# Second decoder layer: output products behind the row copies, absolute sums one per turn, next rows transposed behind the scores

## The chip, the cores and the metric

The kernel runs on one core of a Trainium2 chip. The metric is the device time of one execution in microseconds (us); of several executions the median is given. Besides the times there is a profile of one execution: for each instruction its engine, start, duration and what it waited for. The engines are PE (TensorE, matrix products and transposes), DVE (VectorE), ACT (ScalarE), POOL (GpSimd) and SP (SyncE, which here only issues DMA transfers). Each engine works through its own list of instructions in order; engines wait for each other by semaphores.

## The reference

Two decoder layers on `x` of 16 batches x 112 tokens x 512 values in float32. Each layer adds to `x` a self attention, a cross attention and a feed-forward part, each on the layer-normalized `x`:

```
x = x + L0_attn(ln(x));  x = x + L0_xattn(ln(x), ctx);       x = x + L0_ffn(ln(x))     # mixture of 8 experts + shared
x = x + L1_attn(ln(x));  x = x + L1_xattn(ln(x), ctx, ctx);  x = x + L1_ffn(ln(x))
```

The change lies mainly in the second layer. Its self attention has 16 heads of 32 values, biases and a causal mask. Its cross attention has one head of 512: the queries of a batch attend to 375 context rows and to keys and values made from the batch's own 112 rows. Its feed-forward part quantizes its weights to three values first, and needs for that the mean of each whole matrix's absolute values:

```
scale = mean(|W|) + 1e-8;  q = clip(round(W / scale), -1, 1) * scale
hidden = silu(x @ up.T) * (x @ gate.T);  out = hidden @ down.T
```

## The kernel before

The program is seven stages, one per part (the self- and cross-heads of the first layer's cross attention are two): `stage_attn0`, `stage_fp8_self`, `stage_fp8_cross`, `stage_moe`, `stage_attn1`, `stage_cross1`, `stage_ffn`. `x` stays on chip as 14 tiles of 128 token rows. A recording layer takes every instruction with what it reads and writes, gives it buffers, sets the order on each engine by a model of its own and adds the waits. `manual_schedule` fixes the order on the named engines to the order of the code; `issue_after(i)` puts instructions behind `i` on `i`'s engine only.

**Weights.** One pool of 12 pieces of 128 x 2048 float32 (1 MB, `new_piece`, `load_piece`, L106 to L114) holds every stage's weights, the key tiles `w_kt` of attention 1, and the pieces `w_sum` whose absolute values are summed.

**End of the MoE stage** (L1620 to L1636). While PE runs the shared expert on the last six row tiles, POOL issues 28 gathers (`yg`, L1468, through a tile with five buffers) of the experts' results, and VectorE adds them into `x` (L1634). VectorE's order is fixed here: three additions per step, between the shared expert's own instructions (`h`, L1506, and the addition of its product, L1517). SP meanwhile issues the weights of attention 1 and cross attention 1, and then the pieces for the absolute sums.

**Absolute sums.** `Ternary.add_up(q)` loads three pieces and has ScalarE sum their absolute values (L1835). `stage_attn1` calls it four times before its attention, with the loads placed behind the previous stage's last load on SP (`behind`). The sums are read at the start of `stage_cross1` (`scales`).

**Self attention** (`narrow_attention`, used by both layers). The work is cut into blocks (of 4 batches in attention 1, of 2 to 4 tiles in attention 0) and these into quads: all heads of one batch, or of one tile of 128 rows. The loop has a turn `n` per quad, and one more. In a turn PE computes the scores of quad `n` (L212, L219), VectorE their extremes (`nq_m`, L226), ScalarE the exponentials in four parts `r` (L234), POOL the division (L239); and for quad `n - 1` PE transposes the probabilities (L246), ScalarE copies them out (`ptt`, L251) and PE multiplies them by the values (L259). Between the four parts of a turn stand steps of other work, in the list `now`: a share of the next block's preparation (`before`: transposes of its normalized rows, then query, key and value products), and the two half products of quad `n - 2` with the output weights (`after`), which are put in the middle of the list:

```
now[len(now) // 2 : len(now) // 2] = after
```

PE's and ScalarE's orders are fixed. In the first turn of a block (`group == 0`) two of the next block's row transposes stand ahead of the scores; the rest begin the list. From the second block on, these transposes use the same two PSUM buffers (`mm`) as the products. A transposed row tile is copied out of PSUM by VectorE (`xt`, L190), which also normalizes the rows (`xn`, L145, two buffers, so the third row tile is normalized after the first is transposed).

**Cross attention 1** (`stage_cross1`). For each of four blocks: normalize and transpose its rows (`block_xt`), query and key products for four batches (L1757), and then batch by batch value products (L370), scores (L1780, L1784), a softmax over one row of 487 (maximum L1099, exponentials L1100, division L1791), transposes of the probabilities (L1795), products with context and values (L1805, L1808) and, where a tile of `x` is complete, the output product (L370) and its addition (L1816). The block's transposed rows have one buffer. No engine's order is fixed in this stage. The row transposes and the transposed probabilities share two PSUM buffers (`tr`).

Of the kernel before, what the change touches and what calls it, by code (L numbers as in the profile page):

```python
# [26 lines left out]
GB = 4  # L27
NB = B // GB
# [8 lines left out]
FQ = 4  # L37
# [42 lines left out]
def rows_of(k, g):  # L80

    t = 7 * (g // 2)
    if g % 2:
        rows = [(t + 3, P // 2, P // 2)] + [(t + i, 0, P) for i in (4, 5, 6)]
    else:
        rows = [(t + i, 0, P) for i in range(3)] + [(t + 3, 0, P // 2)]
    return [(k.x[:, t], r, n) for t, r, n in rows]
# [18 lines left out]
def new_piece(k, what, dt=F32):  # L106

    return k.wpool.tile([P, PIECE], dt, tag="w", name=f"w_{what}", bufs=PIECES)


def load_piece(k, what, src):
    piece = new_piece(k, what)
    k.piece_load = k.nc.sync.dma_start(out=piece[:, : src.shape[-1]], in_=src)
    return piece  # L114
# [10 lines left out]
def behind(k):  # L125


    return k.tc.issue_after(k.last_load.ins)
# [30 lines left out]
def block_xt(k, wk, rows):  # L159

    steps = NormedRows(k, wk, rows)
    for i in range(len(rows)):
        steps.transpose(i)
    return steps.xt
# [119 lines left out]
def narrow_attention(k, blocks, aside=None):  # L284

    quads = [(block, group) for block in blocks for group in range(block.groups)]  # L290
    k.evictions = []
    last = len(quads) - 1
    with k.tc.manual_schedule(engines={mybir.EngineType.PE, mybir.EngineType.Activation}):
        for _, step in blocks[0].before(("tr", "mm")):
            step()
        todo, made, done = [], [], 0
        for n in range(len(quads) + 1):
            now = []
            if n <= last:
                block, group = quads[n]  # L300
                if group == 0:
                    done += 1


                    if n == 0:
                        with k.tc.issue_after(k.evictions[2].ins):
                            todo = blocks[done].before(("mm", "tr"))
                    elif done < len(blocks):
                        with k.tc.issue_after(k.xt_copy.ins):
                            todo = blocks[done].before(("mm",))  # L310

                        for _ in range(2):
                            todo.pop(0)[1]()
                    else:
                        todo = []
                budget = sum(cost for cost, _ in todo) / (block.groups - group)
                while todo and (budget > todo[0][0] / 2 or group == block.groups - 1):
                    now.append(todo.pop(0))
                    budget -= now[-1][0]
                made.append(block.quad(group))  # L320
                made[n].scores()

            ahead = n > 0 and done == len(blocks) and not todo and not now
            if n > 1:
                after = quads[n - 2][0].after(quads[n - 2][1])
                now[len(now) // 2 : len(now) // 2] = after
            total, used = sum(cost for cost, _ in now), 0.0
            for r in range(4):
                if ahead:
                    for i in ((0, 1), (2,), (3,), ())[r]:  # L330
                        made[n - 1].transpose_probs(i, ("tr", "mm")[i % 2], i > 1)
                elif n:
                    made[n - 1].transpose_probs(r)
                if n <= last:
                    made[n].exponentials(r)
                while now and used + now[0][0] / 2 < total * (r + 1) / 4 + 1.0:
                    used += now[0][0]
                    now.pop(0)[1]()
                if n:
                    made[n - 1].values(r)  # L340
            for _, step in now:
                step()
            if aside:
                with k.tc.issue_after(k.xt_copy.ins):
                    aside()
        block, group = quads[-1]
        for _, step in block.after(group):
            step()
# [213 lines left out]
class Weights:  # L562
# [56 lines left out]
    def step(self, count):  # L619
        self.ends()  # L620
        self.begin(count)
        self.centers()
        return self
# [1015 lines left out]
class Attn1Block:  # L1639
# [5 lines left out]
    def before(self, tags=("tr",)):  # L1645

        k, wk, nc = self.k, self.wk, self.k.nc
        wq, wkk, wv, _ = (chunks(w, 0, KC, D) for w in k.weights["attn1"])
        rows = rows_of(k, self.g)
        normed = NormedRows(k, wk, rows, tags)  # L1650
        self.qt = wk.tile([P, 4, NT], F32, tag="qt", name="qt", bufs=2)
        self.kt = chunks(new_piece(k, "kt"), 0, 4, NT)
        self.vn = {}

        def transpose(i):
            normed.transpose(i)
            if i == len(rows) - 1:
                for x, first, n in rows:
                    r = slice(first, first + n)
                    nc.gpsimd.tensor_tensor(x[r], x[r], self.bias[r, 1, :], ALU.add)  # L1660

        def wide(dst, w, g, at, sign):
            def product(ps, c):
                nc.tensor.matmul(  # L1664
                    ps, w[:, c, g * P : (g + 1) * P], normed.xt[:, c, :], start=c == 0, stop=c == 3
                )

            def then(ps):
                k.evictions.append(nc.vector.tensor_scalar(
                    dst[:, g], ps, k.vec[:, at + g : at + g + 1], sign / math.sqrt(math.sqrt(32.0)),  # L1670
                    ALU.add, ALU.mult,
                ))

            steps = halves_of(k, [P, NT], "mm", "ps_q", product, then)
            return [(2.0 * NT, step) for step in steps]

        def values(i):
            def product(pv, c):
                nc.tensor.matmul(  # L1679
                    pv, normed.xt[:, c, i * S : (i + 1) * S], wv[:, c, :], start=c == 0, stop=c == 3  # L1680
                )

            def then(pv):
                self.vn[i] = wk.tile([S, D], F32, tag="vn", name="vn", bufs=7)
                nc.vector.tensor_tensor(self.vn[i], pv, self.bias[:S, 0, :], ALU.add)

            return [(2.0 * D, step) for step in halves_of(k, [S, D], "mm", "ps_v", product, then)]

        steps = [(6.0 * n, lambda i=i: transpose(i)) for i, (_, _, n) in enumerate(rows)]
        for g in range(4):  # L1690
            steps += wide(self.qt, wq, g, V_BQ, -1.0)
        for g in range(4):
            steps += wide(self.kt, wkk, g, V_BK, 1.0)
        for i in range(GB):
            steps += values(i)
        return steps
# [33 lines left out]
def stage_attn1(k):  # L1730
    with k.stage("s4", mm=2, tr=1, acc=1, quad=4) as wk:
        mask_to_bf(k, wk, causal_mask(k, wk, S))
        rows = wk.tile([P, 2, D], F32, tag="rows", name="rows")
        k.nc.sync.dma_start(out=rows, in_=k.a["attn1_rows"].partition_broadcast(P))
        with behind(k):
            for q in range(FQ):
                k.ternary.add_up(q)
        at = {}
        narrow_attention(k, [Attn1Block(k, wk, g, rows, at) for g in range(NB)])


def stage_cross1(k):
# [3 lines left out]
    with k.stage("s5", mm=3, tr=2, sc=2, acc=1) as wk:  # L1746
        k.ternary.scales(wk)
        todo, tiles = [(q, m) for q in (0, 1) for m in range(3)], {}
        for g in range(NB):
            xt = block_xt(k, wk, rows_of(k, g))  # L1750
            qt = wk.tile([P, KC, NT], F32, tag="qt", name="qt")
            kt = wk.tile([P, KC, NT], F32, tag="kt", name="kt")
            for n, (dst, w) in enumerate(((qt, wq), (kt, wkk))):
# [11 lines left out]
            for i in range(GB):  # L1765
# [23 lines left out]
                exp_rows(k, pr, ps, sums)  # L1789
                nc.vector.reciprocal(sums, sums)  # L1790
                nc.vector.tensor_scalar(pr, pr, sums, None, ALU.mult)  # L1791
                pt = k.psum.tile([CC, 4, S], F32, tag="tr", name="ps_pt", bufs=2)
                for ch in range(4):
                    n = CC if ch < NCH else S
# [24 lines left out]
class Ternary:  # L1819
# [2 lines left out]

    def __init__(self, k, pool):
        self.k, self.w = k, {}
        self.sums = pool.tile([P, 3, FQ], F32, tag="t_sums", name="t_sums")
        self.s = pool.tile([P, 3], F32, tag="t_s", name="t_s")
        self.half = pool.tile([P, 2, 3], F32, tag="t_half", name="t_half")
# [1 line left out]
    def part(self, q, m):  # L1829
        return self.k.a["ffn_w"][q][:, PIECE * m : PIECE * (m + 1)]  # L1830

    def add_up(self, q):
        for m in range(3):
            w = load_piece(self.k, "sum", self.part(q, m))
            self.k.nc.scalar.activation(w, w, AF.Abs, accum_out=self.sums[:, m, q : q + 1])  # L1835

    def scales(self, wk):
        nc = self.k.nc
# [275 lines left out]
```

## Time and profile before

| | us |
|---|---|
| median of 3 runs (lowest, highest) | 3747.02 (3745.94, 3757.47) |
| the profiled execution's own time | 3740.01 |
| its span, first to last instruction | 3738.2 |
| PE, DVE, ACT, POOL busy in the span | 3577.4, 1798.3, 1425.7, 928.1 |
| last product of the MoE stage ends | 2732.55 |
| turns of attention 1 | 2785.8 to 3056.3 |
| first products of cross attention 1 | 3061.5 |

A line of the timeline reads: start, length, engine, line, operation, output<-inputs, sizes, and how many instructions were merged; in brackets the idle time of the engine before them, and what ended it (`<-` engine, output and line). A line of the table of windows gives the stretch, its length, and then busy time (and instructions) of PE, PE's weight loads, DVE, ACT and POOL, the granted PE clock as a share of full speed, the DMA engines' mean busy share, and GB/s. A line of the chain of waits gives start, length, and the engine or transfer on which the end depended then. PE is busy nearly all the time, so the idle times in front of its instructions are what to read; idle time of other engines costs nothing by itself.

### The profile page before, as it was taken

Reading aid. Unit: us, or ns where it says so; the run is one execution under the profiler, and the core shown is the slowest. Engines: PE = TensorE matmul, PEld = TensorE weight load, DVE = VectorE, ACT = ScalarE, POOL = GpSimd, SP = SyncE. Lnnn points to the kernel's source line nnn. Section 1 sums busy time; section 2 is a strip of 40 time slices with the busy share of each in tenths; the row PEclk is TensorE's granted clock in tenths of the full one; section 3 lists DMA queues with packets and bytes.
Section 4 is the critical chain, followed back from the end, with each engine's and each line's share of the span. In section 5 each row is a group of like instructions: output and inputs, shape, how many; then the busy total and the mean of one; then the engine's idle time right before and its main releaser. Section 6 shows DMA issues by size and latency. Waiting matters only on the chain.

```text
span 3738.2 us, 46258 instructions
## 1 busy us (share of the span) xinstructions
PE 3577.4 (96%) x16450; PEld 2315.5 (62%) x16450; DVE 1798.3 (48%) x3888; ACT 1425.7 (38%) x4133; POOL 928.1 (25%) x1314
## 2 busy tenths in 40 slices
PE   8888899999999999999999999999989999999999
PEld 4546788886666666566666654555544445556888
DVE  5557777876556444544445542111244453214333
ACT  3546766554444444444444430111124431112222
POOL 2335555554222222322222210000232220000000
PEclk9999999999999999999999999999989999999999
DMA  2144333432212111211121115999830022222000
GB/s 88 56 145 150 125 105 118 155 113 87 61 56 73 59 44 51 73 49 49 42 84 44 50 40 165 317 317 319 298 124 12 1 79 78 74 77 82 12 12 17
DMA packets 118117, 364.56 MB, mean 98 GB/s; under 512 B 13280, under 2 KB 33248, under 8 KB 108720
## 3 DMA queue, kind: packets, MB, share of 16 engines
q1 hardware_dynamic: 105504, 332.20, 27.2%
q0 software_dynamic: 5040, 16.52, 1.2%
q10 hardware_dynamic: 7344, 12.89, 0.9%
q8 instruction: 131, 2.15, 0.2%
q14 instruction: 98, 0.80, 0.1%
HBM read 317.09 MB, written 44.47 MB: 97 GB/s over the span
## 4 chain that ended last, share of the span: by engine, by line
PE 70%; DVE 9%; POOL 5%; ACT 3%; issue 2%; DMA 2%; POOLq 0%; SPq 0%; ACTq 0%; DVEq 0%
PE ps_kv L1157 14%; PE ps L1551 6%; PE ps_av L1214 4%; PE ps_s L1189 3%; PE ps_y L1569 3%; PE ps_q L718 3%; PE ps_acc L718 3%; PE ps_u L1933 3%; PE ps_o L370 3%; PE ps_o L1915 3%; PE ps_q L1664 3%; PE ps_g L1933 3%; PE ps_p L1757 3%; PE ps_pt L1204 2%; PE ps_v L1679 1%
## 5 line engine op out<-in xcount | busy, mean ns | idle before, releaser
L1157 PE MATMUL ps_kv<-w_kv,ct 128*125 128x512 f32 x1408 | 636.7, 593 | 0.0
L1157 PEld LDWEIGHTS ps_kv<-w_kv,ct 128*125 128x125 f32 x1408 | 261.9, 188 | 281.8 <-issue 246.9
L559 POOL TENSOR_TENSOR r_o<-r_t,r_m 128x64 fp32r<-128x64 bf16 (+6 forms) x224 | 148.0, 679 | 323.9 <-DVE r_t L557 297.5
L1551 PE MATMUL ps<-w_expert,xgt 128*128 128x448 f32 x560 | 216.4, 539 | 0.7 <-ACT xgt L1543 0.7
L1100 ACT ACTIVATE pr<-ps_s,ex_m 112x375 f32<-112x375 f32 (+1 forms) x272 | 157.4, 580 | 153.9 <-DVE ex_m L1099 145.9
L540 POOL TENSOR_SCALAR cu_v<-cu_v 125x2 f32<-125x2 f32 (+1 forms) x248 | 48.7, 196 | 620.8 <-DVE cu_v L1133 620.8
L541 POOL TENSOR_TENSOR cu_v<-cu_v,mhalf 125x2 f32<-125x2 f32 (+1 forms) x248 | 190.3, 767 | 20.5
L1133 DVE TENSOR_REDUCE cu_v<-sq 125x2 f32<-125x256 f32 (+1 forms) x248 | 118.0, 477 | 160.2 <-ACT sq L1132 160.2
L239 POOL TENSOR_TENSOR pr<-pr,nq_s 112x448 f32<-112x448 f32 (+1 forms) x120 | 118.9, 992 | 291.9 <-DVE nq_s L238 222.7
L234 ACT ACTIVATE pr<-ps_s,nq_m 112x112 f32<-112x112 f32 (+1 forms) x480 | 167.1, 378 | 56.8 <-DVE nq_m L226 56.7
L1099 DVE TENSOR_REDUCE ex_m<-ps_s 112x1 f32<-112x375 f32 (+1 forms) x272 | 148.7, 548 | 79.1 <-PE ps_s L1784 67.1
L1189 PE MATMUL ps_s<-kt,qt 128*112 128x375 f32 x512 | 183.3, 479 | 1.6 <-ACT pr L1100 1.1
L1132 ACT ACTIVATE sq<-ps_kv 125x256 f32<-125x256 f32 x176 | 67.6, 384 | 268.5 <-PE ps_kv L1157 186.5
L534 ACT ACTIVATE qt<-ps_t,turned 128x448 f32<-128x448 f32 (+6 forms) x224 | 116.6, 581 | 130.0 <-PE ps_t L1173 121.9
L1551 PEld LDWEIGHTS ps<-w_expert,xgt 128*128 128x128 f32 x560 | 103.6, 190 | 92.0 <-issue 91.0
L1214 PE MATMUL ps_av<-pt,vn 125*128 125x224 f32 x768 | 159.6, 356 | 0.2
L1189 PEld LDWEIGHTS ps_s<-kt,qt 128*112 128x112 f32 x512 | 90.0, 177 | 100.9 <-issue 60.1
L1214 PEld LDWEIGHTS ps_av<-pt,vn 125*128 125x128 f32 x768 | 142.3, 190 | 9.0 <-ACT pt L1207 4.8
L1204 PEld LDWEIGHTS ps_pt<-ident,pr 112*125 112x125 f32 x768 | 103.3, 191 | 66.2 <-DVE pr L1196 28.2
L1135 DVE TENSOR_TENSOR kn<-ps_kv,cu_v 125x256 f32<-125x256 f32 x176 | 74.7, 425 | 139.8 <-POOL cu_v L541 139.8
L534 ACT ACTIVATE kt<-ps_t,vec 128x375 f32<-128x375 f32 (+7 forms) x240 | 131.5, 588 | 24.9 <-PE ps_t L1179 20.7
L718 PE MATMUL ps_acc<-w_cross,r_o 128*128 128x512 f32 x448 | 135.0, 429 | 3.7 <-POOL r_o L559 3.7
(298 smaller groups left out, 7315.4 us busy)
## 6 DMA issues: line engine op xcount, KB each, us to landing
w_expert<-in_moe_w SPq DMA_DIRECT2D x105, 896.0 KB
ct<-in_ctx_t SPq DMA_DIRECT2D x64, 750.0 KB
xq<-xq_dram SPq DMA_DIRECT2D x42, 512.0 KB
xq<-xx_dram SPq DMA_DIRECT2D x56, 256.0 KB
raw<-in_self_w SPq DMA_DIRECT2D x48, 256.0 KB
w_sum<-in_ffn_w SPq DMA_DIRECT2D x12, 1024.0 KB
cn<-in_ctx SPq DMA_DIRECT2D x16, 750.0 KB
xv<-xv_dram SPq DMA_DIRECT2D x48, 224.0 KB
```

What stands on the lines that cost most here:

```text
L234: nc.scalar.activation(pr[:, j, :], self.ps[:, j, r * t : (r + 1) * t], AF.Exp, bias=self.mx[r][:, j : j + 1], scale=-1.0, accum_out=sums[ ...
L534: k.nc.scalar.activation(dst, src, AF.Identity, bias=cols[:, 1:2], scale=cols[:, 0:1])
L541: nc.gpsimd.tensor_tensor(dst, dst, bc(k.minus_half[: dst.shape[0]], [dst.shape[0], n]), ALU.pow)
L718: k.nc.tensor.matmul(out, lhs(c), w[i][:, c, :], start=first and c == 0 and i == 0, stop=last and c == n - 1 and i == 1,)
L1099: nc.vector.tensor_reduce(mx, src, AX.X, ALU.min)
L1100: nc.scalar.activation(dst, src, AF.Exp, bias=mx, scale=-1.0, accum_out=sums)
L1157: nc.tensor.matmul(pkv, self.ct[:, c, ch * CC : (ch + 1) * CC], w[:, c, :], start=c == 0, stop=c == KC - 1,)
L1189: nc.tensor.matmul(ps, self.heads.qt[self.b][:, h, :], self.kt[:, h // 2, :], start=True, stop=True)
L1204: nc.tensor.transpose(ps[:, h, :], self.pr[:, h, ch * CC : (ch + 1) * CC], k.ident[:S, :S])
L1214: nc.tensor.matmul(av[:, 2 * g : 2 * g + 2, :], self.vn[:, ch, g, :], self.pt[:, ch, 2 * g : 2 * g + 2, :], start=ch == 0, stop=ch == NCH - 1,
L1551: nc.tensor.matmul(pp, self.xt[:, c, :], w[:, c, :], start=c == 0, stop=c == 3)
L1933: nc.tensor.matmul(pp, w[:, c, cols], xt[:, part, c, :], start=c == 0 and part == 0, stop=c == 3 and part == 1,)
```

## The change

Four edits:

1. In `narrow_attention`, in the first turn of a block, the output products go right behind the row transposes that are left, instead of into the middle of the list. The function is shared, so attention 0 gets the same edit; only turns with a following block change.
2. `add_up` becomes one step: sum the piece that is loaded, then load the next. `stage_attn1` passes it to the attention, which calls it at the end of each turn; the loads are no longer placed behind the previous stage's last load. Turn 0 only loads; turns 1 to 12 sum.
3. `Attn1Block` keeps its list of rows, which edit 1 reads.
4. In `stage_cross1` the next block's rows are normalized and transposed after the softmax of the block's last batch is issued, before the transposes of its probabilities, instead of at the head of the next block.

```diff
@@ narrow_attention
             if n > 1:
                 after = quads[n - 2][0].after(quads[n - 2][1])
-                now[len(now) // 2 : len(now) // 2] = after
+
+                at = max(0, len(blocks[done].rows) - 2) if group == 0 and todo else len(now) // 2
+                now[at:at] = after
@@ Attn1Block.before
-        rows = rows_of(k, self.g)
+        rows = self.rows = rows_of(k, self.g)
@@ stage_attn1
-        with behind(k):
-            for q in range(FQ):
-                k.ternary.add_up(q)
         at = {}
-        narrow_attention(k, [Attn1Block(k, wk, g, rows, at) for g in range(NB)])
+        blocks = [Attn1Block(k, wk, g, rows, at) for g in range(NB)]
+        narrow_attention(k, blocks, k.ternary.add_up)
@@ stage_cross1
+        following = block_xt(k, wk, rows_of(k, 0))
         for g in range(NB):
-            xt = block_xt(k, wk, rows_of(k, g))
+            xt = following
...
                 nc.vector.tensor_scalar(pr, pr, sums, None, ALU.mult)
+                if i == GB - 1 and g + 1 < NB:
+                    following = block_xt(k, wk, rows_of(k, g + 1))
                 pt = k.psum.tile([CC, 4, S], F32, tag="tr", name="ps_pt", bufs=2)
@@ Ternary
+        self.left, self.loaded = [(q, m) for q in range(FQ) for m in range(3)], []
...
-    def add_up(self, q):
-        for m in range(3):
-            w = load_piece(self.k, "sum", self.part(q, m))
+    def add_up(self):
+
+        if self.loaded:
+            q, m, w = self.loaded.pop()
             self.k.nc.scalar.activation(w, w, AF.Abs, accum_out=self.sums[:, m, q : q + 1])
+        if self.left:
+            q, m = self.left.pop(0)
+            self.loaded.append((q, m, load_piece(self.k, "sum", self.part(q, m))))
```

In the order that results, the output products move in two turns of attention 0 (6 and 10) and two of attention 1 (4 and 8). In cross attention 1 the sixteen transposes of the next rows stand in one piece between the scores and the transposed probabilities after batches 3 and 11; after batch 7 four of them stand ahead of the two products that follow the scores there, and twelve behind them.

## The prediction

> **What bounds the kernel now.** The page's first part, read first:
>
> ```profile
> PE 3577.4 (96%) x16450; PEld 2315.5 (62%) x16450; DVE 1798.3 (48%) x3888; ACT 1425.7 (38%) x4133; POOL 928.1 (25%) x1314
> ```
>
> PE has 160.8 us idle (3738.2 less 3577.4) and the change takes no PE work away, so it can win only idle PE time, or time at a low PE clock. I then read PE's timeline where the diff acts, then whatever PE waited for.
>
> Seam MoE to attention, PE then VectorE:
>
> ```profile
> 2723.78 8.77 PE L1513 MATMUL ps_o<-w_shared,h 64*128 64x512 f32 x18 [0.68 <-DVE h L1506]
> 2739.53 1.97 PE L155 MATMUL ps_xt<-ident,xn 128*128 128x128 f32 x8 [6.97 <-DVE xn L145]
> ```
> ```profile
> 2720.66 0.56 DVE L1506 TENSOR_TENSOR h<-sl,ps 128x384 f32<-128x384 f32 x1 [1.53 <-ACT w_sum L1835]
> ...
> 2737.41 0.69 DVE L1634 TENSOR_TENSOR x<-x,yg 128x512 f32<-128x512 f32 x1 [0.69 <-DMA yg<-y_dram,g_slot]
> 2738.20 0.69 DVE L1517 TENSOR_TENSOR x<-x,ps_o 128x512 f32<-128x512 f32 x1
> ```
>
> PE ends at 2732.55 and stands 6.97 us, because VectorE, whose order is fixed here, still adds gathered rows. The chain of waits has why (start, length), and the table of windows what the DMA engines did (last columns: PE clock, DMA share, GB/s):
>
> ```profile
> 2693.10 3.67 DMA yg<-y_dram,g_slot
> ...
> 2727.43 9.88 DMA yg<-y_dram,g_slot
> ```
> ```profile
> 2732.00:2738.00 6.00, 0.56 (x2) 0.00 (x0) 2.73 (x5) 3.07 (x3) 0.00 (x0) 0.67 1.02 416
> ```
>
> The last gather needs 9.88 us among the 12 MB of `w_sum` loads. Attention 1, first turns of a block (two rows of PE, then VectorE):
>
> ```profile
> 2860.79 3.19 PE L1664 MATMUL ps_q<-xt,w_attn 128*128 128x448 f32 x4 [2.53 <-DVE xt L190]
> ...
> 2939.79 1.77 PE L1664 MATMUL ps_q<-xt,w_attn 128*128 128x448 f32 x4 [2.54 <-DVE xt L190]
> ```
> ```profile
> 2857.61 2.20 DVE L226 TENSOR_REDUCE nq_m<-ps_s 112x4 f32<-112x448 f32 x4
> 2859.73 1.01 DVE L190 COPY xt<-ps_xt 128x512 f32<-128x512 f32 x2
> ```
>
> The `xt` copies stand behind the four reductions. ScalarE there (the two extremes of its idle time at the start of a turn), and what it would take over:
>
> ```profile
> 2857.48 0.54 ACT L251 COPY ptt<-ps_pt 112x448 f32<-112x448 f32 x1 [5.25 <-PE ps_pt L246]
> ...
> 3019.39 0.97 ACT L251 COPY ptt<-ps_pt 112x448 f32<-112x448 f32 x2 [2.52 <-PE ps_pt L246]
> ```
> ```profile
> L1835 ACT ACTIVATE w_sum<-w_sum x12: 1910/1911/1915, 2679.6 to 2743.1; 128x2048 f32<-128x2048 f32 x12
> ```
>
> Cross attention, seams after batch 3 and batch 11:
>
> ```profile
> 3136.31 0.76 PE L1795 MATMUL ps_pt<-ident,pr 112*125 112x112 f32 x4 [2.25 <-DVE pr L1791]
> ...
> 3150.38 22.07 PE L1757 MATMUL ps_p<-xt,w_cross 128*128 128x448 f32 x58 [1.10 <-DVE xt L190]
> ```
> ```profile
> 3311.33 0.68 PE L1795 MATMUL ps_pt<-ident,pr 112*125 112x112 f32 x4 [2.25 <-DVE pr L1791]
> ...
> 3322.50 24.32 PE L1757 MATMUL ps_p<-xt,w_cross 128*128 128x448 f32 x64 [1.10 <-DVE xt L190]
> ```
>
> From the end of the scores to the next block's products these take 16.32 and 13.42 us. The work is the same; the first ran at a lowered clock:
>
> ```profile
> 3136.00:3140.00 4.00, 3.69 (x19) 3.30 (x20) 1.31 (x4) 0.44 (x1) 0.00 (x0) 0.60 0.17 69
> ...
> 3311.00:3316.00 5.00, 4.48 (x38) 4.20 (x39) 1.34 (x4) 0.44 (x1) 0.00 (x0) 1.00 0.16 65
> ```
>
> **The change part by part**, against the profiled execution (3740.01 us; span 3738.2).
>
> 1. *Absolute sums, ScalarE.* Twelve of 1.91 us plus a 0.19 us read leave the MoE tail; one goes to the end of turns 1 to 12 of attention 1. From there to the next turn's first copy ScalarE idles 2.52 to 5.25 us, over the 2.0 needed: cost 0. Without that cover each turn would lose up to 2.0 (24 in all). Each load is issued a turn (15 to 22 us) ahead; the chain shows at most 9.88 for 256 KB in the crowd, and attention 1 moves almost no other data.
>
> 2. *Their loads, SP.* In the built order the rows' load (L1734) passes the eleven loads it stood behind; it waits for the last `h` (L1506), about 2721 instead of 2731.83. POOL's bias additions waited 11.75 for it but also follow the transposes: 0. One `w_sum` load has a free slot and follows; the next waits for the shared expert's last product, the rest for sums or key tiles inside attention 1. The first raw load for cross attention now waits for the last key products (2983, was 2837); the context loads behind it wait until 3045 anyway: 0. So 1.5 MB, not 12, meets the last gathers: at the window's 416 GB/s, with their own 1 MB, 6 us from 2721, before PE's end. POOL issues a gather each 1.25 us and is not late.
>
> 3. *The seam.* PE loses the 0.68 wait (h behind a sum) and ends at 2731.87; the last addition starts 0.04 later, and from its start to the first transpose stays 1.33 (2738.20 to 2739.53): 2733.24 instead of 2739.53, **-6.3**. Bounds: a last gather from 2723 that again takes 9.88 ends VectorE some 1.8 later (-4.5); the gathers as late as now would leave 0, which the ten loads now held back make unlikely. I take -6.3, as the nearest row is the 3.67 landing. Clock: 0.80 over 2745 to 2760 costs 3.0; bounds 0 and -3, taken **-1.0**, since the transposes after the gap keep PE sparse.
>
> 4. *Output products in a block's first turn.* Turn 4: their PSUM slots ("mm", two) are held by the transposes, so they wait for the first `xt` copy (2860.35) instead of the second: **-0.5**, bounds 0 and -1.9 (if the slow 3.19 of the row becomes 1.77). Turn 8: values (0.33) and probability transposes (0.43) come first and fill the gap, then the products from 2939.2; the turn's second values go from 2945.79 to 2944.44: **-1.35**. The same line moves two turns of attention 0: at 138.6 PE waits 2.88 for a copy; another 0.85 of work comes ahead of it: **-0.85**; the other has no gap: 0.
>
> 5. *Next rows transposed behind the scores.* Sixteen transposes, four copies and two normalizations move between scores and probability transposes. Counted from the scores' end with the rows' durations (maximum 0.67, copy 0.42 or 0.6, normalization 0.45): two transposes at once, the third at 1.6, the fourth at 2.75, probabilities scaled at 3.2, transposed at 3.9 (now 2.25) since VectorE's copies precede; values from 4.85, then 0.65 for the copy that transposes covered, products at 12.75 instead of 13.42: **-0.7** (batch 11) and **-3.6** (batch 3, 16.32, of which 2.9 is clock). After batch 7 the softmax is already covered by output products; there the one `xt` buffer holds the copies until the value product has read it, probabilities are transposed about 2.3 later and one end gap goes: **+0.6**. Bounds for all three: +1 (no gain, copies later by one) to -6.
>
> Sum -6.3 -1.0 -0.5 -1.35 -0.85 -0.7 -3.6 +0.6 = -13.7: 3726.3 for the profiled execution. The runs' median, 3747.02, lies 7.0 above; the same difference gives **3733.3**.
>
> The clock rows: after a PE gap of 2.53 us it was 0.57 (2860 to 2864), after 2.25 it was 0.60 (3136), yet after 2.54 (2939) and 2.25 (3311) it stayed 1.00. [...]
>
> **The rivals.**
> - *Clock by chance.* If low clock comes by phase and not from the gap, the 2.9 and 1.0 are not won: -9.8, **3737.2**. For: equal gaps with both outcomes. Against: low clock is seen only next to gaps.
> - *Gathers end the stage all the same* (latency or row buffers, not traffic): of 7.3 only 0.7 to 4.5 stays: about -9, **3738**. For: five row buffers; against: landings grow from 3.67 to 9.88 with traffic.
> - *The new small gaps lower the clock.* Between scores and values PE now works 2.1 of 4.85 us; at half clock as at 3136 each seam costs 2.9: three give -13.7 + 8.7 = -5, **3742**.
> - *Slower: a sum holds ScalarE.* Sums stand ahead of the next turn's copy (L251), which PE's values need. It decides once a sum starts over 0.5 us late in the tightest turn, or its load needs more than a turn. Two us uncovered in twelve turns give +24 -13.7: **3757**. Against: the cover rows.
>
> **How the numbers follow.** Forecast 0.45, chance clock 0.2, late gathers 0.12, lowered clock 0.13, slower 0.1. 0.3% is 11.2 us, about what a measurement of this kernel can tell from no change. The forecast falls under 3735.8 in nine of ten, the next three in one of five: 0.5 faster, 0.4 within, 0.1 slower. The range goes from -17 (item 3's and 4's other bounds), with 6 for an execution as fast as the profiled one, to the lowered clock and 4 more: 3724 to 3746.
>
> **What would show it.** First transpose of attention 1 about 1.4 us after the last shared product, and a last gather under 6 us; ScalarE's first copies of turns not later against PE; first-turn gaps 2.0 and 1.2; scores to products 12.8 after batches 3 and 11. Wrong if PE's wait there is still for gathered rows, or PE waits for ScalarE in attention 1.

## The result, and the profile after

Over 20 runs the changed kernel takes a median of 3735.31 us (3729.11 to 3752.41); the kernel before, on the same chip, 3748.41 us (3740.35 to 3785.69, 20 runs). The ratio is 0.9962, 95% interval 0.9949 to 0.9974: 14.2 us less (9.7 to 19.1). Forecast were 13.7 us. The profiled executions differ by less: spans 3730.9 and 3738.2 us, -7.3, because the one profile of before is of a quick execution (3740.01 us, 8.4 under its median) and that of after is nearer its own (3732.72, 2.6 under). The sections below show one cause of such differences between executions, and that the sum came out for reasons that the forecast had only in part. One of the ten executions of a later measurement of the changed kernel took 4565 us at a mean granted clock of 0.75, where all others had 0.98 or 0.99; the ratio there leaves it out.

The page after; PE's work is the same to 0.3 us:

```profile
PE 3577.7 (96%) x16450; PEld 2317.0 (62%) x16450; DVE 1797.2 (48%) x3888; ACT 1422.7 (38%) x4133; POOL 928.2 (25%) x1314
```

**Seam from the mixture of experts to attention 1.** PE's timeline after, then VectorE's, then SP's:

```profile
2720.27 11.44 PE L1515 MATMUL ps_o<-w_shared,h 128*128 128x512 f32 x24
2735.11 1.97 PE L155 MATMUL ps_xt<-ident,xn 128*128 128x128 f32 x8 [3.39 <-DVE xn L145]
```
```profile
2727.18 0.69 DVE L1636 TENSOR_TENSOR x<-x,yg 128x512 f32<-128x512 f32 x1 [2.39 <-DMA yg<-y_dram,g_slot]
2731.18 1.29 DVE L1636 TENSOR_TENSOR x<-x,yg 128x512 f32<-128x512 f32 x2 [3.31 <-DMA yg<-y_dram,g_slot]
...
2733.78 0.69 DVE L1519 TENSOR_TENSOR x<-x,ps_o 128x512 f32<-128x512 f32 x1
```
```profile
2721.57 0.33 SPq L1736 DMA_DIRECT2D rows<-in_attn_rows  x1
2721.95 10.12 SPq L113 DMA_DIRECT2D w_sum<-in_ffn_w  x2
```

The wait of the shared expert for a sum is gone: its 24 products run in one piece. PE then stands 3.39 us (6.97 before, about 1.4 forecast), still for gathered rows. The chain of waits and the windows of the DMA engines (last columns: PE clock, DMA share, GB/s) say why:

```profile
2719.39 3.62 DMA yg<-y_dram,g_slot
...
2725.24 7.11 DMA yg<-y_dram,g_slot
```
```profile
2724.00:2728.00 4.00, 4.00 (x10) 1.53 (x10) 1.38 (x2) 0.00 (x0) 2.37 (x4) 1.00 1.01 336
```

The rows (0.5 MB) and the first `w_sum` (1 MB) are issued at 2721.6 and 2722.0 and fill the DMA engines just when the last gathers run: the gather that starts at 2719.39, ahead of them, takes 3.62 us, the last one, among them, 7.11. It lands at 2732.35, after PE's last product.

**The sums in the turns.** The group of sums, with its busy time, its mean, and the idle time in front of it:

```profile
L1840 ACT ACTIVATE w_sum<-w_sum 128x2048 f32<-128x2048 f32 x12 | 23.2, 1936 | 0.0
```

They never wait for their loads. Ahead of the first copy of each turn ScalarE still idles, 1.98 us or more up to the copy at 2966, but only 0.68 and 0.62 at 2981 and 3010: the cover is nearly used up there. No wait of PE in the turns ends with one of these copies, so PE is not held.

**Output products in a block's first turn** (attention 1's turns 4 and 8, attention 0's turn 6; PE):

```profile
2854.30 1.98 PE L1714 MATMUL ps_o<-w_attn,at 128*128 128x512 f32 x4 [2.20 <-DVE xt L190]
2931.26 3.70 PE L1714 MATMUL ps_o<-w_attn,at 128*128 128x512 f32 x8 [1.08 <-DVE xt L190]
```
```profile
141.00 0.43 PE L259 MATMUL ps_av<-ptt,vn 128*32 128x128 f32 x8 [2.02 <-ACT ptt L251]
```

The waits were 2.53, 2.54 and 2.88 us.

**Cross attention.** PE after batch 3, where the next products start at 3136.38, and after batch 7:

```profile
3125.35 0.63 PE L155 MATMUL ps_xt<-ident,xn 128*128 128x128 f32 x4 [0.66 <-DVE xn L145]
3126.46 0.63 PE L155 MATMUL ps_xt<-ident,xn 128*128 128x128 f32 x4 [0.49 <-DVE xn L145]
3127.35 0.68 PE L1798 MATMUL ps_pt<-ident,pr 112*125 112x112 f32 x4 [0.26 <-DVE xt L190]
3128.61 0.92 PE L1808 MATMUL ps_av<-ptt,cn 125*128 125x112 f32 x6 [0.58 <-ACT ptt L1802]
...
3212.23 0.66 PE L155 MATMUL ps_xt<-ident,xn 128*128 128x128 f32 x4 [0.34 <-DVE xt L190]
3213.37 0.43 PE L155 MATMUL ps_xt<-ident,xn 64*128 64x64 f32 x4 [0.49 <-DVE xn L145]
...
3215.14 1.62 PE L1808 MATMUL ps_av<-ptt,cn 125*128 125x112 f32 x6 [0.58 <-ACT ptt L1802]
```

After batch 3 the seam is 12.67 us from the scores' end to the next products (16.32 before) at full clock. After batch 7 the same six value products take 1.62 us instead of 0.92: one seam has lost a low clock, and another now has one. Counted in the same way, from the end of the scores, that seam is 20.80 us, 18.16 before; the one after batch 11 is 15.76, 13.42 before. In this pair of executions cross attention as a whole loses 1.8 us (351.7 to 353.5, from its first product to the first product of the last stage).

### The profile page after: what moved, and what is told of

It reads as the page before. It is cut to its first block, busy times and chain, and to the rows that moved or that the text cites. A ratio compares the mean times of both kernels' runs of the same rounds, so it can differ in the third digit from the quotient of the medians.

```text
span 3730.9 us, 46245 instructions
## 1 busy us (share of the span) xinstructions
PE 3577.7 (96%) x16450; PEld 2317.0 (62%) x16450; DVE 1797.2 (48%) x3888; ACT 1422.7 (38%) x4133; POOL 928.2 (25%) x1314
## 4 chain that ended last, share of the span: by engine, by line
PE 69%; DVE 9%; POOL 5%; ACT 3%; issue 3%; DMA 2%; POOLq 0%; SPq 0%; ACTq 0%; DVEq 0%
PE ps_kv L1159 14%; PE ps L1553 6%; PE ps_av L1216 4%; PE ps_s L1191 3%; PE ps_y L1571 3%; PE ps_q L720 3%; PE ps_acc L720 3%; PE ps_o L372 3%; PE ps_u L1941 3%; PE ps_o L1923 3%; PE ps_g L1941 3%; PE ps_q L1666 3%; PE ps_pt L1206 2%; PE ps_p L1758 2%; PE ps_v L1681 1%
```

## Experiments

Seams are read as above, from the end of the scores to the next products. "Before-type" means the part in question as in the kernel before. A range in brackets behind a time is its 95% interval. Every run has one profile; where an experiment has one execution only, its time is not compared.

### Each part alone

Sums alone (before, with the second half of the diff):

```diff
-        with behind(k):
-            for q in range(FQ):
-                k.ternary.add_up(q)
...
+        narrow_attention(k, blocks, k.ternary.add_up)
...
```

> The kernel before with the absolute sums moved alone (one per turn of attention 1), nothing else. Both theories of the seam give its gain here and nowhere else: the first transpose of attention 1 at about 2735 us, 4.4 earlier than before, with PE's gap there 3.4 us and a last gather of about 7 us. First theory, of the forecast: the rest of this part is free, so the kernel's time is 4.4 to 5.4 us less than before (1.0 of it clock). Rival: the seam also held the clock down in the turns behind it, or the sums cost ScalarE something in the turns; then the time differs from -5 by 2 us or more, and the first products of cross attention show it: they come 4.4 to 5.4 earlier by the first theory.

Measured: 0.9973 (0.9957 to 0.9989), -10.1 us (-4.1 to -16.1). First transpose 2737.24, PE's gap 3.81, last gather 9.26 us from 2723.95. The turns are not longer (attention 1, from its first transpose to the first products of cross attention, takes 320.4 us; 322.0 in the profile of before), and those products start at 3057.66, 3.9 us earlier than before, where 4.4 to 5.4 were expected. So this profile shows no cost of the sums in the turns. The interval of the time holds the expected gain near its low end; the rest of the 10.1 us is not explained by this profile.

Output products alone:

```diff
-                now[len(now) // 2 : len(now) // 2] = after
+                at = max(0, len(blocks[done].rows) - 2) if group == 0 and todo else len(now) // 2
+                now[at:at] = after
...
```

> The kernel before with the output products alone placed behind the rows' copies in a block's first turn, in attention 0 and attention 1. By the changed kernel's trace against the one before: wait ahead of the products in turn 4 2.2 us instead of 2.53, in turn 8 1.1 instead of 2.54, in attention 0 2.0 instead of 2.9; sum -2.65, so the time is 2.7 us less than before. Rival: gaps shortened below some length no longer lower the clock, which would add up to 1.4 in turn 4 (the 3.19 us group at 1.77) and 2 or more in all; then -4 to -6.

Measured: 0.9979 (0.9960 to 0.9999), -7.9 us (-0.4 to -15). The three waits are 2.20, 1.08 and 2.03 us, as in the changed kernel; attention 1 takes 317.0 us. The interval holds both theories; the traces favour the second for turn 8. With the old order (wait 2.54) the products behind it took 1.77 us in the profile of before, but 3.27 to 3.36 us, at half clock, in all five other profiles with that order; with the new one (wait 1.08) the clock was full in every profile. Turn 4 keeps both outcomes with either order: the clock was low there in two of six profiles with the old one and in five of eight with the new one.

This run's seam to attention 1, which it leaves as before, showed a second way in which sums cost time (PE, then ScalarE):

```profile
2724.34 1.13 PE L1514 MATMUL ps_o<-w_shared,h 128*128 128x512 f32 x2 [1.74 <-DVE h L1507]
2726.86 10.47 PE L1514 MATMUL ps_o<-w_shared,h 64*128 64x512 f32 x18 [1.39 <-DVE h L1507]
2743.48 1.97 PE L155 MATMUL ps_xt<-ident,xn 128*128 128x128 f32 x8 [6.15 <-DVE xn L145]
```
```profile
2721.32 1.91 ACT L1836 ACTIVATE w_sum<-w_sum 128x2048 f32<-128x2048 f32 x1 [7.12 <-DMA w_sum<-in_ffn_w]
2723.14 0.19 ACT L1836 ACTIVATION_READ_ACCUMULATOR w_sum<-w_sum 128x1 f32 x1
2723.23 0.98 ACT L1506 ACTIVATE sl<-ps 128x384 f32<-128x384 f32 x2
```

A sum stands 7.12 us for its load, and the shared expert's `sl`, which needs no load, stands behind it on ScalarE. From the end of the last up products to the first transpose this seam takes 22.6 us, against 19.0 in the profile of before.

Next rows behind the scores, alone:

```diff
+        following = block_xt(k, wk, rows_of(k, 0))
...
-            xt = block_xt(k, wk, rows_of(k, g))
+            xt = following
...
+                if i == GB - 1 and g + 1 < NB:
+                    following = block_xt(k, wk, rows_of(k, g + 1))
```

> The kernel before with the next batches' rows transposed behind the scores alone, in cross attention. Work without clock: seams after batches 3 and 11 are 12.7 us from scores to products instead of 13.4, the one after batch 7 is 0.6 longer: -0.8 us in all. Three theories differ by the clock: (a) low clock is due to the 2.25 us gap of before, which is gone: it appears in no seam now, -3.7; (b) low clock falls on the seams by chance in both kernels: seams of 12.7 or 15.8, each in some executions, median -0.8; (c) the small gaps now standing there lower it more often: two of three seams at 15.8, +2 to +5.

Measured: 0.9996 (0.9979 to 1.0013), -1.5 us (-7.9 to +4.9). Seams: after batch 3 12.67 at full clock, after batch 7 20.81 and after batch 11 15.72, both with low clock. Theory (a) falls, since low clock appears in two seams that have the new order. The interval of the time still holds its -3.7; that this part is worth next to nothing rests on the seams of several profiles, which follow below.

### The seam: traffic or ScalarE

All loads, hardly any sums (before, each sum over one column of 2048, the rest of the summing left out):

```diff
-            self.k.nc.scalar.activation(w, w, AF.Abs, accum_out=self.sums[:, m, q : q + 1])
+            self.k.nc.scalar.activation(w[:, :1], w[:, :1], AF.Abs, accum_out=self.sums[:, m, q : q + 1])
```

> The kernel before, with each absolute sum taken over one column of its 2048 (most of this part of the computation is left out); all twelve 1 MB loads stay. Theory of traffic: ScalarE's 23 us of sums are gone but the last gather is as late as before, about 9 to 10 us, PE's gap at the seam 5 to 7 us, first transpose of attention 1 at 2738 to 2740; only the 0.68 us wait of the shared expert for a sum goes. Rival, ScalarE's sums made the seam late (they hold what VectorE's additions wait for): gap under 3.4, first transpose near 2735 or earlier.

Measured: last gather 8.03 us, PE's gap 3.87, first transpose 2746.83 in an execution whose shared expert was 9.7 us late already; from the last up products 16.6 us. Between the two expectations: the gather is as slow as the theory of traffic says, but the gap is shorter, and the shared expert still waits (1.40 us), since `sl` still stands behind a sum that waits for its load. This one execution alone does not settle it.

All sums, one load (before, one piece summed twelve times, the other eleven left out):

```diff
-            w = load_piece(self.k, "sum", self.part(q, m))
+            if not self.w:
+                self.w[0] = load_piece(self.k, "sum", self.part(q, m))
+            w = self.w[0]
...
```

> The kernel before, with one piece loaded and summed twelve times (eleven of the twelve pieces of this part are left out), so ScalarE's 23 us of sums stay in the tail of the mixture of experts and 11 MB of loads are gone. Theory of traffic: last gather 4 to 6 us (the rows' 0.5 MB is left), PE's gap 1.4 to 3 us. Rival, ScalarE's sums: gap 5 to 7 us as before.

Measured, PE:

```profile
2729.14 11.44 PE L1513 MATMUL ps_o<-w_shared,h 128*128 128x512 f32 x24
2741.94 1.11 PE L155 MATMUL ps_xt<-ident,xn 128*128 128x128 f32 x8 [1.37 <-DVE xn L145]
```

The gap is 1.37 us with all of ScalarE's sums in place, so without the loads the sums cost nothing. From the last up products to the first transpose this seam takes 12.64 us, against 16.6 with the loads and hardly any sums, and 18.9 to 22.6 with both: the loads start it, and the sums that wait for them add to it (how much rests on one execution). The rows' 0.5 MB is still loaded there, issued at 2730.44, 10.1 us before PE's end as in the changed kernel, and costs nothing; so what is left in the changed kernel should be the first `w_sum` load.

The changed kernel with a quiet seam:

```diff
-        rows = wk.tile([P, 2, D], F32, tag="rows", name="rows")
+        rows = chunks(new_piece(k, "rows"), 0, 2, D)
...
-            self.loaded.append((q, m, load_piece(self.k, "sum", self.part(q, m))))
+            first = (q, m) == (0, 0)
+            w = new_piece(self.k, "sum") if first else load_piece(self.k, "sum", self.part(q, m))
+            if first:
+                self.k.nc.scalar.dma_start(out=w, in_=self.part(q, m))
+            self.loaded.append((q, m, w))
```

> The changed kernel with two things more: the shift rows of attention 1 are loaded into a weight piece that is free early, right behind the cross weights, and the first load of the sums is issued from ScalarE's queue in the first turn of attention 1. So no bulk load runs during the last gathers. Theory (the 1.5 MB of rows and first sums still delay the last gather): its time falls from 7.1 to about 3.8 us, PE's gap from 3.39 to about 1.4, the first transpose comes at about 2733.2 instead of 2735.1, and the time is 2 us less than the changed kernel, -16 against before. Rival (the last gather is late for another reason, as latency, row buffers or the order of VectorE's additions): gather still 6 to 7 us, gap above 3, no time won against the changed kernel (-14).

Measured: 0.9960 (0.9943 to 0.9977), -15.0 us (-8.6 to -21.4), which does not tell the two expected times apart. Its chain of waits at the seam, and the windows in which the gathers end (PE, PE's weight loads, DVE, ACT, POOL, PE clock, DMA share, GB/s):

```profile
2719.96 11.29 PE ps_o L1515 x24
2731.25 0.02 issue
2731.27 0.69 DVE x L1519
2731.96 0.13 DVE mask_bf L365
2732.09 0.47 DVE xn L145
2732.55 0.04 issue
2732.60 0.67 PE ps_xt L155 x4
```
```profile
2724.00:2728.00 4.00, 4.00 (x10) 1.48 (x9) 2.46 (x5) 0.00 (x0) 2.26 (x4) 1.00 0.68 189
2728.00:2732.00 4.00, 3.23 (x8) 0.93 (x6) 1.85 (x4) 0.00 (x0) 0.00 (x0) 1.00 0.00 0
```

No gather is left in the chain: it goes from PE's last product over one addition and one normalization to the transpose, and the gap is 1.37 us. That is the forecast's gap, and the theory of traffic holds. From the last up products to the first transpose, over all traces but the one with hardly any sums: before-type 18.9, 19.0, 22.1 and 22.6 us (mean 20.6; in those of 22 a late load holds `sl` for longest); sums moved 14.2 to 15.1 (mean 14.7, four traces); quiet, or with one load, 12.64 in all five. The seams of this run in cross attention, whose order is that of the changed kernel, are 12.67, 22.37 and 14.30 us.

### The clock at the seams

The quiet seam again, with the next rows behind the scores after batch 3 only:

```diff
-            xt = following
+            xt = following if g in (0, 1) else block_xt(k, wk, rows_of(k, g))
...
-                if i == GB - 1 and g + 1 < NB:
+                if i == GB - 1 and g + 1 == 1:
```

> The kernel with the quiet seam (rows early, first sum's load in ScalarE's queue), and the next rows transposed behind the scores only after batch 3; after batches 7 and 11 the order is that of before. Theory that the clock follows the local order of work: seam after batch 3 12.7 us at full clock, after batch 7 18.2 at full clock (20.8 to 22.4 where the change moved the rows), after batch 11 13.4 to 16.4; so 2.6 us or more faster than the kernel with the quiet seam, about -18 against before. Rival, that a low clock is due about once in so many us whatever the order: the full clock after batch 3 is paid back after batch 7 or 11, so those take 20 or more, or 16, and the time is not under that of the quiet seam (-15).

Measured: 0.9936 (0.9913 to 0.9959), -24 us (-15 to -33). Seams 12.66, 18.15 and 16.40. After batch 7 the full clock is kept, as the theory of the local order says. The time is further below than the -18 expected, but its interval holds that.

The mirror of it, the changed kernel with the next rows behind the scores after batch 7 only:

```diff
-            xt = following
+            xt = following if g in (0, 2) else block_xt(k, wk, rows_of(k, g))
...
-                if i == GB - 1 and g + 1 < NB:
+                if i == GB - 1 and g + 1 == 2:
```

> The changed kernel, with the next rows transposed behind the scores only after batch 7. Theory of the local order: seam after batch 3 16.3 to 16.5 us with the clock halved (2.25 us gap of before), seam after batch 7 20.8 or more with the clock lowered among its small gaps, as in the changed kernel. Rival, a low clock due at intervals: having fallen after batch 3, it stays away after batch 7, which then takes 18.8 (18.16 of before and 0.6 of work).

Measured: after batch 3 16.33 with low clock, after batch 7 19.18 at full clock, after batch 11 13.42. Here the rival was the nearer one: the very order that had a low clock after batch 7 in four profiles has none in this one. Neither theory holds alone. The run also gives the work without the clock's part: 19.18 less 18.16, +1.0 us (forecast: +0.6).

So I measured the clock itself. The low stretches of this part of the program are 3.42, 6.84, 10.24, 13.66 or 17.08 us long, one to five times 3.413, and start whole multiples of 3.413 apart (in before, 2733.98, 2792.00, 2860.28, 3061.66, 3136.76: 17, 20, 59 and 22 of them; the 402.78 us from the first to the last, over these 118, give the 3.413). Cutting twelve of the traces, from 17 to 19 us on, into such windows from one of their own edges gives 13,016 windows, none with a mixed clock: 12,638 at 1.00 and 378 at 0.50. Before's seam after batch 3 on its grid (window, length, PE busy, clock, DMA share, GB/s), then the same gap in the run with one load, where no low clock followed:

```profile
3133.34:3136.75 3.41, 1.16 (x12) 1.00 0.67 218
3136.75:3140.17 3.42, 3.42 (x19) 0.50 0.03 12
3140.17:3143.58 3.41, 3.41 (x18) 0.50 0.00 0
```
```profile
3132.22:3135.63 3.41, 1.89 (x12) 1.00 0.41 133
3135.63:3139.05 3.42, 2.49 (x20) 1.00 0.30 115
```

The gap is 2.25 us in both. In the first it lies inside one window, which is busy for 34% and is followed by two windows at half clock; in the second a window edge cuts it, and both windows are busy for more than half. Over the twelve traces, for windows at full clock:

| PE busy in a window | next window at half clock |
|---|---|
| under 40% | 166 of 166 |
| 40 to 60% | 76 of 195 |
| 60 to 70% | 3 of 202 |
| 70% and over | 0 of 12,063 |

A window at half clock busy for under 80% was always followed by another (97 of 97); of those over 80%, 245 of 281 were followed by full clock. The changed kernel's seams after batch 3 and after batch 7:

```profile
3122.98:3126.39 3.41, 2.34 (x20) 1.00 0.66 222
3126.39:3129.81 3.42, 2.51 (x18) 1.00 0.03 10
```
```profile
3211.73:3215.14 3.41, 1.92 (x15) 1.00 0.00 0
3215.14:3218.55 3.41, 3.41 (x16) 0.50 0.02 5
```

The second of them (3211.73 to 3215.14) holds three gaps of 0.34, 0.49 and 0.58 us and is followed by half clock; the gaps of 0.66, 0.49, 0.26 and 0.58 after batch 3 are split by an edge and are not. So a few small gaps went with a low clock, as one of 2.25 us did, after batch 7, where they lay in one window (56% busy), and not after batch 3, where an edge split them (69 and 73%). So far this is a reading of traces. A test that changes PE's busy share there and keeps the order otherwise: the kernel before with useless work in the gap.

```diff
+                av = k.psum.tile([P, KC, S], F32, tag="acc", name="ps_av", bufs=1)
+                if i == GB - 1 and g in (0, 2):
+                    for n in range(12):
+                        nc.tensor.transpose(av[:S, n % 4, :], k.ident[:S, :S], k.ident[:S, :S])
...
-                av = k.psum.tile([P, KC, S], F32, tag="acc", name="ps_av", bufs=1)
```

> The kernel before, with twelve transposes of the identity (work that nothing uses) in PE's 2.25 us gap ahead of the probability transposes after batches 3 and 11; PE's order is otherwise that of before. Theory of windows by PE's busy share: no window there is under half busy any more, the clock stays full, both seams take 13.4 to 13.6 us in the profile; in the six and seven executions seen so far with that gap they took 15.9 and 15.1 on average, so the time is about 4 us less than before, although PE works more. Rival, that the low clock is not the gap's doing: seams of 15 to 16.5 in most executions stay, and the time is that of before or, by the added work, up to 1 us more.

Measured: 0.9988 (0.9975 to 1.0001), -4.5 us (-9.4 to +0.4). Both seams at full clock, 13.42 and 13.43 us; PE's rows and the windows after batch 3:

```profile
3140.44 1.31 PE L1795 MATMUL ps_av<-ident 112*112 112x112 f32 x12
3142.86 0.68 PE L1799 MATMUL ps_pt<-ident,pr 112*125 112x112 f32 x4 [1.10 <-DVE pr L1791]
```
```profile
3140.15:3143.56 3.41, 2.31 (x22) 1.00 0.67 225
3143.56:3146.97 3.41, 3.21 (x29) 1.00 0.02 5
```

Without the 1.31 us of filler the first of these windows would be busy for 29%. PE has more work, and cross attention takes 347.2 us instead of 350.2 to 352.2 in the five before-type profiles (mean 351.4). The interval of the time just includes zero; the seams show it. With the old order and no filler, the clock was low after batch 3 in five of six profiles and after batch 11 in six of eight.

The changed kernel once more, and the two best versions beside it on one chip; the last is the first-seam version with the filler after batch 11:

```diff
...
+                if i == GB - 1 and g == 2:
+                    for n in range(12):
+                        nc.tensor.transpose(av[:S, n % 4, :], k.ident[:S, :S], k.ident[:S, :S])
...
```

> The changed kernel itself once more, beside the two below on one chip. Against before: -14 us as in its first runs (-9 to -19). In its profile, by the theory that the clock is set window by window (fixed windows of 3.41 us; one in which PE is busy under about half makes the next run at half clock): every low stretch is a whole number of 3.41 us long, starts at a whole number of 3.41 us from every other, and follows a window under 0.6 busy; the seam after batch 3 is at full clock or loses 1.5 to 3 by where the windows fall. Rival, a low clock set off by a gap's own length: stretches start at the ends of gaps, anywhere.

> The kernel with the quiet seam and the next rows behind the scores after batch 3 alone, once more, on one chip with the changed kernel. By the traces so far it wins against the changed kernel 2.0 us at the seam to attention 1 and about 2.6 after batch 7: -19 against before, 4 to 5 us under the changed kernel. Rival: both gains are lost again to where the clock's windows fall; no difference, -14.

> The kernel with the quiet seam and the next rows behind the scores after batch 3 alone, and the same filler in the gap after batch 11. Seam after batch 11 at 13.4 to 13.6 us (16.4 without the filler in the one execution seen), after batch 3 12.7, after batch 7 18.2; time 1.5 to 3 us under the kernel without the filler, about -21 against before. Rival: seam after batch 11 still 15 to 16.5, no gain.

Measured, all against the same runs of before: changed kernel 0.9964 (0.9951 to 0.9977), -13.5 us, median 3737.66; first seam only 0.9952 (0.9935 to 0.9969), -18.0 us, median 3731.22; with the filler 0.9950 (0.9936 to 0.9964), -18.7 us, median 3729.80. Low stretches of the changed kernel between 2680 and 3330 us: 13.66, 6.84, 3.42, 6.84 and 3.44 us, on the grid. Its seams: 12.66, 20.82 and 12.67; the first-seam version's 12.66, 18.16 and 15.05; with the filler 12.67, 18.16 and 13.42. Both versions are faster than before. That they are also faster than the changed kernel, by 4.5 and 5.2 us here, their intervals, which overlap, do not show. The four seams of these profiles add up to 2.5 and 4.1 us less than in the changed kernel's; against the mean over all profiles with that order of the seams it is some 5 and 6 us.

## Why the prediction was right, and where it was not

**Step 1, sums cost nothing:** right; the group above has no waits in front of it, and PE none for the copies behind it. The cover was thinner than the forecast's 2.52 to 5.25 us against 2.0: 0.62 us was left in the tightest turn. The rival by which a sum holds ScalarE did not come true after the change. Something like it had been true before: in two of four before-type seams, where `sl` stands longest behind a late sum, the seam is some 3.4 us longer (22.1 and 22.6 against 18.9 and 19.0); the one profile of before showed only the 0.68 us wait.

**Step 2, the loads:** the order on SP was as forecast (rows at 2721.57, then one `w_sum`). The failing sentence is "1.5 MB, not 12, meets the last gathers: at the window's 416 GB/s, with their own 1 MB, 6 us from 2721, before PE's end". The DMA engines were full (share 1.01) but moved 336 GB/s, and the last gather, started at 2725.24, took 7.11 us: it landed at 2732.35, not near 2727, and 0.6 us after PE's end. By the prediction's own sign (PE's wait still for gathered rows, a last gather not under 6 us) this step failed. The cause is not that of the rival, latency or row buffers, but the traffic that was left, as the quiet seam shows.

**Step 3, the seam:** -6.3 forecast, -4.4 in the pair of profiles, the bound that was named (-4.5). The mechanism was right, the quiet seam gives the forecast's 1.37 us gap. Against the mean of the before-type seams the change wins 5.9 us, since their mean is longer than the one profile shows; the forecast's size thus came out by two errors of opposite sign, which is luck. The clock term there (-1.0) was of the right kind: the first low stretch is 17.08 us in the profile of before, 10.24 and 13.66 in the two of the changed kernel.

**Step 4, output products:** forecast -0.5, -1.35 and -0.85; the waits fell by 0.33, 1.46 and 0.86. Missing was the clock behind turn 8's wait, some 1.5 us in five of six profiles, which the profile of before happened not to have. Attention 1 as a whole: mean 320.8 us in six profiles with the old order (318.7 to 323.5), 318.9 in eight with the new (316.0 to 321.1); seven of these eight also have the sums moved, so that the 1.9 is not the products' alone.

**Step 5, cross seams:** wrong in sum. -3.6 after batch 3 came out (-3.65), -0.7 after batch 11 and +0.6 after batch 7 did not (+2.3 and +2.6 in the pair; +1.0 of the latter is work). Step 5 took the low clock of one execution as a property of that seam and the full clock of the others as a property of theirs. Cross attention's mean is 351.4 us in five before-type profiles and 351.2 in four with all rows moved: -0.2, where -3.7 was forecast; the run of that part alone says -1.5 (-7.9 to +4.9).

The rivals: low clock by chance and new small gaps that lower it are both half true, as two faces of the windows. That the 2.9 us go with the gap, as step 5 had it, holds in so far as with the gap filled the low clock was gone in both seams (13.42 and 13.43 us), and as in the twelve traces all 166 windows at full clock and under 40% busy were followed by half clock. It does not hold for every execution: the same 2.25 us, cut by a window's edge, left two windows busy for 55 and 73%, and no low clock followed.

**The sum.** By the traces (the wait in attention 0, means of several profiles for the rest): -5.9, -1.9, -0.9 and -0.2, together -8.9 us, against -14.2 (-9.7 to -19.1) and -13.5 measured. The missing 5 us are not located; four to eight profiles a part carry an error of a few us, and nothing was found ahead of the seam that the change could move. The record has a hint to their kind. The profile of before has a mean granted clock of 0.985, the two of the changed kernel 0.986. Over the executions whose clock is on record, before has 0.9834 (76 of them) and the changed kernel 0.9850 (29); side by side on one chip 0.9829 and 0.9852. So the executions differ more in clock than the profiles do, by 0.0006 to 0.0013. An estimate from that, with the 0.50 of all 378 low windows: 0.001 of 3740 us is 7.5 us more at half clock, at most 3.7 us of time, which makes 2 to 5 us; in which stage they lie is not shown. The prediction was right in time and range, right in the places of the seam, the sums and the products, and wrong on what cross attention gives. That 13.7 came so near to 14.2 is luck: 3.7 of it were due to cross attention, which gave about nothing, and about 5 us of the gain are not located in any of its terms.

## What to carry to other kernels

The end of the mixture of experts, which waited for gathers, got shortest with all bulk loads away from the last ones, not with most of them away: 1.5 MB of the 12 still cost 2 us here (14.7 against 12.64). In ScalarE's order a sum that stood 7.12 us for its load held back `sl`, which needs no load; look at what stands behind each waiting instruction. And a low PE clock seen in one profile may belong to that execution's phase (after batch 3 five of six profiles had it, after batch 11 six of eight): average such a term over several profiles, or fill the gap (1.31 us of transposes took the seams to 13.4 us).

## What the runs showed of the hardware

In the twelve traces that were cut into windows the granted PE clock changed only between windows of 3.413 us (in before 402.78 us over 118 of them), on a grid of the execution's own, and was 1.00 or 0.50 in each (12,638 and 378 windows). By PE's busy share in a window at full clock, the next one was at half clock after all 166 under 40%, after 79 of the 397 from 40 to 70%, where the share alone does not decide it, and after none of the 12,063 from 70% on. A gap of 2.25 us was followed by half clock after batch 3 in five of six profiles, and not in the one in which an edge cut it into windows of 55% and 73%. With useless transposes in the gap (twelve of 112x112, 1.31 us) the clock stayed full in the three seams where they stood (13.42 and 13.43 us in the kernel before, 13.42 in the last version); the window after batch 3 in the kernel before shows 2.31 us busy with them.

The window edges do not fall quite at random on the seams: in eleven of twelve traces the scores after batch 3 end 0.07 to 0.89 us after an edge, and the twelfth, 1.90 after one, is the execution whose 2.25 us gap did no harm. That work between two low stretches takes a fixed time from a window's edge would explain it, and why a low clock after batch 3 goes with a full one after batch 7; this was only argued.
